# Two-layer graph network on one core: the sums of source and target rows formed by an accumulating gather, and five smaller edits

## The chip, the cores and the metric

The kernel runs on one NeuronCore of a Trainium2 chip. The metric is the time of one execution on the device, in microseconds (us). A core has several engines that run their own instruction lists in order: TensorE (PE in the profile) multiplies matrices into accumulators in PSUM, VectorE (DVE) and ScalarE (ACT) work on rows, GpSimd (POOL) here mostly issues transfers whose addresses come from a list of indices, and SyncE (SP) issues the large loads of weights. They wait for each other by semaphores.

## The reference

There are 625 nodes with 1024 features and 10000 edges from src to dst, sorted by dst. Two layers follow each other, and each has a graph part, a linear attention, and a feed-forward part. Cut to what matters here:

```
xn = layernorm(x)
# layer 0, graph attention: 4 heads of 64, with a self loop for every node
h = rmsnorm(xn) @ W_down
xl, xr = h @ Wl, h @ Wr
msg = xl[src] + xr[dst]
e = einsum('ehd,hd->eh', where(msg > 0, msg, 0.2 * msg), att)
alpha = softmax of e over the edges that have the same dst
g = segment_sum(alpha * xl[src], dst) @ W_up
# linear attention: 16 heads, phi = elu + 1
k, v, q = phi(xn @ Wk), xn @ Wv, phi(xn @ Wq)
m = (q @ (k^T v)) / (q @ sum(k)) @ Wo
x = x + g + m
x = x + ternary_ffn(layernorm(x))
# layer 1
xn = layernorm(x)
x = x + sage(sage(xn)) + linear_attention(xn)   # sage: mean over edges, two products
x = x + attention_and_moe(layernorm(x))         # 8 experts, 2 of them per token
```

## The kernel before, in words

The nodes are 5 tiles of 125. The order of instructions on every engine is written out by hand: a stream object takes for each piece of work its TensorE part and the work that follows it on the other engines, and puts that follow-up one or two steps later. A whole attempt is run once with a plain softmax (the exponentials are not shifted by a maximum); tests collected in `inside` decide at the end whether a second, shifted attempt has to run. With the given data it doesn't.

Layer 0's first stage does the following together.

TensorE computes the keys, values, queries and answers of the linear attention (class `LinearAttention`, L240 to L335). In between, `count` (L418 to L464) multiplies one-hot rows of the edges (bf16, made by VectorE) for 79 blocks of 128 edges into accumulators `pct`, so that a matrix CT of edge counts per pair of nodes results. Two node halves are packed in one number as low + 4096 high. The 79 blocks go in three pieces (up to 27, 53 and 79); after each piece VectorE decodes the accumulators (L448 to L460).

The edge scores are computed in groups of G = 2 columns of 128 edges; 39 groups are full, and the 40th is one column of 16 edges. For a group g POOL fetches rows of xl by src into `ga` and rows of xr by dst into `gb` with indirect transfers (`gather`, L573 to L580). VectorE adds both (L586), applies the leaky relu (L557), multiplies by `att` (L558), reduces per head (L559) and limits the result (L561). ScalarE takes the exponential (L565). POOL scatters it into a table in DRAM at place (src, dst) (`scatter`, L589 to L595). The self loops (`self_loops`, L601 to L608) do the same with rows that are on chip, one node tile at a time, and store the results on the table's diagonal; they also copy xl into `xl1`, which has a 65th column of ones per head.

The pace of the edge work is a plan. `work(us)` is called after every piece of TensorE work with its planned time, and for every 7.6 us it issues one beat g: the self loops of tile g-1 (beats 1 to 5), the exponential of group g-4, the scoring of group g-3, and then column by column on POOL the two gathers of group g and the scatter of group g-5.

When the attention is done, the product px with the output weights follows (L668); VectorE sums the ternary weights (`weight_sums`, L707), POOL loads the table back by target tile (`load_table`, tb), `weigh` multiplies it by the counts (L743), and TensorE forms pg, the weighted sums of the xl1 rows, of which the 65th column is the softmax denominator. Then come seven rounds p = 0 to 6 (`for p in range(NT + 2)`), in which the graph sums of tile p and the feed-forward part of tile p-1 alternate with a `spacer`: two pieces of px in the early rounds, and keys and values of layer 1's attention (`lin1`) from p = 3 on. A key piece writes pk into a small accumulator (`ps1`, of which there are two), adds the bias on VectorE (kb, L247), and takes exp and relu on ScalarE (ke, L249).

After this, layer 1's query loop runs over 8 blocks m; TensorE computes pq, pd and po, and beside them VectorE and ScalarE make the normalized rows of layer 1 and split them into a high and a low part, half a tile at a time (`rows_of`, ten calls, L1072 and L1045 to L1047); at one m VectorE also forms the inverses of the degrees (`inverses`, L1037 to L1041). The rest of the program, from about 850 us on, is the SAGE layers, attention and experts.

Of the kernel before, what the change touches and what calls it, by code (L numbers as in the profile page):

```python
# [33 lines left out]
NB_MIN = 10  # L34
FAR = -1.0e30
LIMIT = 60.0
LEAST, MOST = 1.0e-22, 1.0e25
MAGIC = 12582912.0
BIG = 1.5 * 2.0**35

# [12 lines left out]
def attempt(ctx: ExitStack, tc: tile.TileContext, w: dict, out: bass.AP, shifted: bool):  # L53
# [26 lines left out]
    nc.vector.memset(blockmask[0:64, 0:64], 1.0)  # L80
    nc.vector.memset(blockmask[64:128, 64:128], 1.0)

    inside = const.tile([128, 3], FP, name="inside")
    nc.vector.memset(inside, 1.0)

    def test(col, src, n, pool):
# [128 lines left out]
    class LinearAttention:  # L215


        def __init__(self, xnT, names, bq, work, rows_on):
            self.xnT, self.names, self.work, self.rows_on = xnT, names, work, rows_on
            self.bq = mix.tile([128, KC], FP, tag="bq", name="bq", bufs=2)  # L220
            rows_on.dma_start(out=self.bq, in_=bq)
            self.kv = []
# [15 lines left out]
        def key(self, t):  # L238
            kf, bk, wk = self.kf, self.bk, self.wk

            def pe():
                hold["pk", t] = ps1("pk")
                group(hold["pk", t][:P], [(self.xnT[:, k, nodes(t)], wk(k)) for k in range(KC)])

            def after():
                kb = mix.tile([P, 512], FP, tag="kb", name="kb", bufs=1)
                nc.vector.tensor_tensor(kb, hold.pop(("pk", t))[:P], bk[:P], op=ALU.add)  # L247
                ke = mix.tile([P, 512], FP, tag="ke", name="ke", bufs=1)
                nc.scalar.activation(ke, kb, AF.Exp)  # L249
                nc.scalar.activation(kb, kb, AF.Relu)  # L250
                hold["k", t] = ke, kb

            def after2():
                ke, kb = hold.pop(("k", t))
                nc.vector.scalar_tensor_tensor(kf[:, t, :], ke, 1.0, kb, op0=ALU.min, op1=ALU.add)

            do(None, pe, after, after2)
            self.work(6.9)

        def value(self, t):  # L260
            v, bv, wv = self.v, self.bv, self.wv

            def pe():
                hold["pv", t] = ps1("pv")
                group(hold["pv", t][:P], [(self.xnT[:, k, nodes(t)], wv(k)) for k in range(KC)])

            def after():
                nc.vector.tensor_tensor(v[:, t, :, 0:128],  # L268
                                        hold.pop(("pv", t))[:P].rearrange("p (a b) -> p a b", a=4),
                                        bv[:P].rearrange("p (a b) -> p a b", a=4), op=ALU.add)  # L270

            do(None, pe, after)
            self.work(6.9)
# [64 lines left out]
    with ExitStack() as st0:  # L338
# [8 lines left out]
        with ExitStack() as edges:  # L347
# [51 lines left out]

            pad(xnT)  # L400
            nc.vector.memset(xl1[:, :, :, 64:65], 1.0)

            counting = [(lo, hi, t) for lo, hi in ((0, 27), (27, 53), (53, EN)) for t in range(lo, hi)]
            part = dict(done=0, held=0)
            made_ahead = []

# [10 lines left out]
            def count():  # L419
# [20 lines left out]
                def decode():  # L440
                    for j in range(0, NT, 2):
                        js = slice(j, min(j + 2, NT))
                        n = js.stop - j
                        low, high, v = CT[:, js, 0:HN], CT[:, js, HN:NP], part["pc"][:P, js, :HN]
                        low_r, high_r = CTr[:, js, 0:HN], CTr[:, js, HN:NP]
                        u = pool.tile([P, 2, HN], FP, tag="u", name="u", bufs=1)[:, 0:n, :]

                        nc.vector.tensor_scalar(u, v, 1728.0, BIG, op0=ALU.subtract, op1=ALU.add)  # L448
                        nc.vector.tensor_scalar(u, u, BIG, None, op0=ALU.subtract)
                        if lo == 0:  # L450
                            nc.vector.tensor_tensor(low_r, v, u, op=ALU.subtract)
                            nc.vector.tensor_scalar(high_r, u, 1.0 / 4096, None, op0=ALU.mult)
                        else:
                            nc.vector.scalar_tensor_tensor(high_r, u, 1.0 / 4096, high, op0=ALU.mult, op1=ALU.add)
                            nc.vector.tensor_tensor(u, v, u, op=ALU.subtract)
                            nc.vector.tensor_tensor(low_r, low, u, op=ALU.add)
                    if hi == EN:

                        for s in range(NT):
                            nc.vector.tensor_tensor(CTr[:, s, nodes(s)], CT[:, s, nodes(s)], ident[:P, :P],  # L460
                                                    op=ALU.add)
# [90 lines left out]

            def score(dst, m, n, p):

                nc.vector.scalar_tensor_tensor(m, m, 0.2, m, op0=ALU.mult, op1=ALU.max)  # L557
                nc.vector.tensor_tensor(m, m, att[0:p].unsqueeze(1).to_broadcast([p, n, 256]), op=ALU.mult)  # L558
                nc.vector.tensor_reduce(dst, m.rearrange("p t (h e) -> p t h e", h=4), AX.X, ALU.add)  # L559
                if not shifted:  # L560
                    nc.vector.tensor_scalar(dst, dst, LIMIT, None, op0=ALU.min)  # L561
# [10 lines left out]
            def gather(g, j):  # L572
                lo, n, p = groups[g]  # L573
                if j == 0:
                    ab[g] = [pool.tile([128, G, 256], FP, tag=k, name=k, bufs=4) for k in ("ga", "gb")]
                if j < n:
                    for dst, src, ix in ((ab[g][0], xl_d, si), (ab[g][1], xr_d, di)):
                        nc.gpsimd.indirect_dma_start(  # L578
                            out=dst[0:p, j, :], out_offset=None, in_=src[:, :],
                            in_offset=bass.IndirectOffsetOnAxis(ap=ix[0:p, lo + j:lo + j + 1], axis=0))  # L580

            def score_group(g):
                lo, n, p = groups[g]
                a, b = ab.pop(g)
                m = a[0:p, 0:n, :]
                nc.vector.tensor_tensor(m, m, b[0:p, 0:n, :], op=ALU.add)  # L586
                score(es[0:p, lo:lo + n, :], m, n, p)

            def scatter(g, j):  # L589
                lo, n, p = groups[g]  # L590
# [4 lines left out]
                        in_=es[0:p, lo + j, :], in_offset=None)  # L595

            own = pool.tile([P, NT, 4], FP, name="own")

            diagonal = table[0:N * (N + 1), :].rearrange("(s d) h -> s d h", d=N + 1)[:, 0, :]

            def self_loops(t):  # L601

                m = pool.tile([P, 1, 256], FP, tag="xd", name="gs", bufs=1)
                nc.vector.tensor_tensor(m[:, 0, :], xlr[:, t, 0:256], xlr[:, t, 256:512], op=ALU.add)
                score(own[:, t:t + 1, :], m, 1, P)
                exp(own[:, t:t + 1, :])
                nc.vector.tensor_copy(xl1[:, t, :, 0:64], xlr[:, t, 0:256].rearrange("p (h e) -> p h e", h=4))
                rows_dma(nc.scalar, diagonal[nodes(t), :], own[:, t, :])  # L608


# [1 line left out]

            def work(us):
                beat["us"] += us
                while beat["us"] >= 7.6 * beat["g"] and beat["g"] < len(groups) + 5:
                    g = beat["g"]
                    beat["g"] += 1
                    if 1 <= g <= NT:
# [6 lines left out]
                    for j in range(G):  # L625
                        if g < len(groups):
                            gather(g, j)
                        if g >= 5:
                            scatter(g - 5, j)

            work(0.0)
            states = []
# [55 lines left out]
            nc.sync.dma_start(out=wu, in_=w["W_up"].rearrange("(k p) n -> p k n", p=128))  # L688
            bo = [lin.bias(w["L0_bo"], c, tag) for c, tag in enumerate(("bk_t", "bv_t"))]
            do.flush()  # L690
            while beat["g"] < len(groups) + 5:
                work(8.0)

        xpool = ctx.enter_context(tc.tile_pool(name="xpool", bufs=1, side="right", reuse_waits="tile"))
        x = xpool.tile([P, NT, D], FP, name="x")
# [265 lines left out]
        for p in range(NT + 2):  # L961
# [11 lines left out]
            if p == 0:  # L973
                xnT1 = bigT("xnT1")
                nc.gpsimd.memset(xnT1[:, :, N:NP], 0.0)
                lin1 = LinearAttention(xnT1, ("L1_Wq", "L1_Wk", "L1_bk", "L1_Wv", "L1_bv"), w["L1_bq"],
                                       lambda us: None, nc.gpsimd)
            if p < NT:
                sums(p)
            if 1 <= p <= NT:  # L980
# [37 lines left out]
    def degrees():  # L1018
# [8 lines left out]
        def after():  # L1027
            nc.vector.tensor_scalar(halves(dinv), hold["pdeg"][:, :, :HN], 1.0, None, op0=ALU.max)
            if not shifted:
                most = sage.tile([128, 1], FP, name="most")  # L1030
                nc.vector.tensor_reduce(most, dinv, AX.X, ALU.max)
                nc.vector.tensor_scalar(inside[:, 1:2], most, 4095.0, None, op0=ALU.is_le)

        do(None, pe, after)

# [40 lines left out]
    for m in range(KC - 1):  # L1076
        lin1.query(m + 1)
        lin1.answer(m, oT)
        for _ in range(2 if m < 4 else 1):
            if rows_left:  # L1080
                rows_of(*rows_left.pop(0))
        if m == 5:
            inverses()
    assert not rows_left
    for name in ("b1", "L1_bo"):
# [513 lines left out]
    def ranks():  # L1599
        hold["prt"] = ps1("prt")  # L1600
        group(hold["prt"][:P, 0:NT * NE], [(before, flat)])
        group(hold["prt"][:P, NT * NE:2 * NT * NE], [(ones[:P, :P], flat)])
        group(hold["prt"][:P, 2 * NT * NE:2 * NT * NE + 3], [(ones[:, :P], inside)])

    do(None, ranks)
    ptot = hold["prt"][:, NT * NE:2 * NT * NE]
# [48 lines left out]
    nc.vector.tensor_reduce(exp_f, blk, AX.X, ALU.add)  # L1655
    meta = pool.tile([P, NB + 2], I32, name="meta")
    within = pool.tile([P, 1], FP, name="within")
    nc.vector.tensor_reduce(within, hold["prt"][:P, 2 * NT * NE:2 * NT * NE + 3], AX.X, ALU.add)
    nc.vector.tensor_scalar(meta[:, NB + 1:NB + 2], within, -1.0, 384.0, op0=ALU.mult, op1=ALU.add)
    nc.vector.tensor_scalar(meta[:, 0:NB], exp_f, float(NE - 1), None, op0=ALU.min)  # L1660
    nc.vector.tensor_copy(meta[:, NB:NB + 1], ends[3][:, NE - 1:NE])
    hidden(3)
# [71 lines left out]
    rest(NB_MIN)  # L1734
    again = None
    if not shifted:
        again = nc.values_load(meta[0:1, NB + 1:NB + 2], min_val=0, max_val=384,
                               skip_runtime_bounds_check_because="384 less three sums of up to 128 ones and zeros")


    with tc.manual_schedule(engines={mybir.EngineType.PE, mybir.EngineType.DVE, mybir.EngineType.Pool}):
# [121 lines left out]
```

## Time and profile before

| what | value |
|---|---|
| median of 3 runs | 2243.34 us (2241.93 to 2249.37) |
| the profiled execution's own time | 2241.98 us |
| its span in the profile | 2240.2 us |
| mean granted TensorE clock | 0.977 |
| TensorE busy | 2124.3 us, 95% |
| VectorE busy | 754.2 us, 34% |
| ScalarE busy | 193.5 us, 9% |
| POOL busy | 346.7 us, 15% |

The span is what the profile covers; 1.8 us of the execution lie outside of it. Times of instructions are in us from the span's start. In the profile a line of a timeline gives the start, the duration, the engine, the line of the kernel, the operation, what it writes and reads, and in brackets how long the engine stood idle before it and what ended that. A line of a group of instructions gives the number of instructions, their busy time in us and the mean in ns, and the idle time before them. In the slices of the span each digit is the busy share in tenths of one fortieth, 56 us. The TensorE clock may be granted in part only, which lengthens its products.

### The profile page before, as it was taken

What the parts mean: (1) busy time and instruction counts of PE and PEld (TensorE: products, weight loads), DVE (VectorE), ACT (ScalarE), POOL (GpSimd) and SP (SyncE); (2) the same over time, 40 slices, a digit from 0 to 9 for tenths busy, and PEclk for the clock granted to TensorE, in tenths of its full rate; (3) what the DMA queues carried; (4) which work ended last, traced back from release to release, by engine and by line L of the source; (5) the groups of instructions that cost most, each with busy time, mean ns of one, the idle gap of its engine ahead of it and who ended that gap; (6) DMA issues with size and microseconds to landing.
All of it is one profiled execution on the core that took longest, in us unless ns stands there. A gap on an engine that the chain in (4) does not pass through costs nothing. (4 is left out here: it accounts for less than half of the span.)

```text
span 2240.2 us, 17398 instructions
## 1 busy us (share of the span) xinstructions
PE 2124.3 (95%) x6934; PEld 1214.5 (54%) x6934; DVE 754.2 (34%) x1265; ACT 193.5 (9%) x349; POOL 346.7 (15%) x351
## 2 busy tenths in 40 slices
PE   7997889798899989999999999999999999999998
PEld 5564455354554657764445767556754444444443
DVE  4878668666421580000113124322111111111112
ACT  2000011011110210000000111110000000000000
POOL 1667767400000040010000000110000000000010
PEclk9998999898899999999999999999999999999999
DMA  9452252431122110231212111030198997998742
GB/s 282 126 179 64 65 187 86 111 89 43 38 85 75 47 48 1 75 141 38 75 38 103 38 38 38 19 103 33 62 337 320 333 331 278 326 332 294 268 147 93
DMA packets 145849, 301.63 MB, mean 135 GB/s; under 512 B 12370, under 2 KB 22436, under 8 KB 145754
## 3 DMA queue, kind: packets, MB, share of 16 engines
q1 hardware_dynamic: 123412, 243.18, 30.4%
q0 software_dynamic: 17664, 47.47, 7.1%
q10 hardware_dynamic: 4678, 9.72, 1.4%
q8 instruction: 58, 0.95, 0.2%
q14 instruction: 37, 0.30, 0.0%
HBM read 277.49 MB, written 22.84 MB: 134 GB/s over the span
## 5 line engine op out<-in xcount | busy, mean ns | idle before, releaser
L129 PE MATMUL pu<-w,xgT 128*128 128x512 f32 x768 | 333.9, 593 | 1.9 <-DVE xgT L1157 1.9
L129 PEld LDWEIGHTS pu<-w,xgT 128*128 128x128 f32 x768 | 144.0, 190 | 174.8 <-issue 172.0
L129 PE MATMUL pyb<-w,hb 128*128 128x512 f32 x384 | 174.3, 598 | 2.5 <-ACT yb L104 2.1
L129 PE MATMUL pq<-xnT,w 128*128 128x313 f32 x512 | 143.2, 440 | 11.0 <-DVE v L268 9.7
L129 PE MATMUL pk<-w,xnT 128*125 128x512 f32 x320 | 141.0, 593 | 4.7 <-DVE x L909 4.7
L129 PE MATMUL pv<-w,xnT 128*125 128x512 f32 x320 | 140.7, 592 | 1.2 <-ACT xnT L925 1.2
L129 PE MATMUL p<-tT,w 128*128 128x313 f32 x512 | 136.3, 428 | 0.4 <-DVE tT L1157 0.4
L129 PEld LDWEIGHTS pq<-xnT,w 128*128 128x128 f32 x512 | 99.8, 196 | 54.1 <-DVE v L268 10.5
L1697 DVE TENSOR_TENSOR su<-pu,su 128x512 f32<-128x512 f32 x24 | 16.6, 691 | 314.6 <-ACT su L1696 314.6
L129 PEld LDWEIGHTS pyb<-w,hb 128*128 128x128 f32 x384 | 69.8, 189 | 90.9 <-issue 74.8
L129 PEld LDWEIGHTS p<-tT,w 128*128 128x128 f32 x512 | 96.8, 190 | 37.9 <-issue 1.2
L129 PEld LDWEIGHTS pk<-w,xnT 128*125 128x125 f32 x320 | 59.3, 187 | 78.7 <-issue 72.0
L129 PEld LDWEIGHTS pv<-w,xnT 128*125 128x125 f32 x320 | 59.4, 188 | 72.4 <-issue 70.5
L592 POOL DMA_INDIRECT table<-es,at x79 | 88.3, 1118 | 63.7 <-DMA table<-es,at 32.6
L1680 POOL DMA_INDIRECT xg<-rows_d,slots x12 | 11.4, 947 | 524.7 <-PE pxg L1687 449.0
L578 POOL DMA_INDIRECT gb<-xr_d,di x79 | 81.7, 1034 | 24.1 <-issue 24.1
L578 POOL DMA_INDIRECT ga<-xl_d,si x79 | 80.1, 1014 | 30.9 <-issue 20.1
L668 PE MATMUL px<-w,oT 128*125 128x512 f32 x160 | 75.6, 629 | 8.1 <-DVE oT L333 6.5
L1047 DVE TENSOR_TENSOR z<-pz,z 125x512 fp32r<-125x512 f32 x10 | 6.9, 692 | 196.8 <-ACT z L1045 196.8
L129 PE MATMUL px<-w,hT 128*125 128x512 f32 x160 | 70.3, 592 | 0.0
L129 PE MATMUL px<-w,oT 128*125 128x512 f32 x160 | 70.3, 592 | 0.0
L129 PE MATMUL ph<-meanT,w 128*128 128x313 f32 x256 | 70.1, 426 | 0.0
(359 smaller groups left out, 2572.0 us busy)
## 6 DMA issues: line engine op xcount, KB each, us to landing
w<-in_eW_dram SPq DMA_DIRECT2D x144, 1024.0 KB
w<-in_L_Wk_dram SPq DMA_DIRECT2D x8, 1024.0 KB
w<-in_L_Wv_dram SPq DMA_DIRECT2D x8, 1024.0 KB
w<-in_L_Wq_dram SPq DMA_DIRECT2D x8, 1024.0 KB
w<-in_L_Wo_dram SPq DMA_DIRECT2D x8, 1024.0 KB
w<-in_W_self_dram SPq DMA_DIRECT2D x8, 1024.0 KB
w<-in_W_neigh_dram SPq DMA_DIRECT2D x8, 1024.0 KB
w<-in_sW_dram SPq DMA_DIRECT2D x8, 1024.0 KB
```

What stands on the lines that cost most here:

```text
L129: nc.tensor.matmul(dst, lhsT=lhsT, rhs=rhs, start=(i == 0), stop=(i == len(pairs) - 1))
L578: nc.gpsimd.indirect_dma_start(out=dst[0:p, j, :], out_offset=None, in_=src[:, :], in_offset=bass.IndirectOffsetOnAxis(ap=ix[0:p, lo + j:l ...
L592: nc.gpsimd.indirect_dma_start(out=table[:, :], out_offset=bass.IndirectOffsetOnAxis(ap=at[0:p, lo + j:lo + j + 1], axis=0), in_=es[0:p, l ...
L668: nc.tensor.matmul(hold["px", t][:P, c, :], lhsT=oT[:, k, nodes(t)], rhs=wo[c](k), start=(k == 0), stop=False)
L1047: nc.vector.tensor_tensor(low, src, high.bitcast(FP), op=ALU.subtract)
L1680: nc.gpsimd.indirect_dma_start(out=xg, out_offset=None, in_=rows_d[:, :], in_offset=bass.IndirectOffsetOnAxis(ap=slots[:, b:b + 1], axis=0))
L1697: nc.vector.tensor_tensor(su, pu[:, 0, :], su, op=ALU.mult)
```

## The change

It has six parts. (1) `gb` goes; the rows of xr are added by a transfer with an add of its own, `add_targets`, into `ga`, which has 6 buffers instead of 4. It is issued one beat after the plain gather of the same group. (2) The leaky relu of m is written as 0.2 m + 0.8 max(m, 0). Per edge only the second part is left: one operation, max with zero and multiply by att (scaled by 0.8 beforehand). Of the first part, what belongs to the target cancels in the softmax; what belongs to the source becomes a weight exp(0.2 att . xl) on the source's row in `xl1`, computed in `self_loops`. A test on this weight is added. (3) The counts of all 79 blocks stay in the accumulators and are decoded once; the test of it is extended. (4) The keys and values of `lin1` use the larger accumulators (`ps2`, three of them). (5) The scatter comes 4 instead of 5 beats after the gather. (6) The query loop of layer 1 takes three `rows_of` per step while there are any (3, 3, 3, 1) instead of two and then one (2, 2, 2, 2, 1, 1), and the inverses come at m = 4 instead of 5.

The diff, cut to its core:

```diff
-LEAST, MOST = 1.0e-22, 1.0e25
+LINEAR = 20.0
+LEAST, MOST = 1.0e-22, 1.0e16
...
-    inside = const.tile([128, 3], FP, name="inside")
+    inside = const.tile([128, 4], FP, name="inside")
...
-                hold["pk", t] = ps1("pk")
+                hold["pk", t] = ps2("pk")[:, 0, :] if self.large else ps1("pk")
...
-                hold["pv", t] = ps1("pv")
+                hold["pv", t] = ps2("pv")[:, 0, :] if self.large else ps1("pv")
...
+            if not shifted:
+                nc.vector.tensor_scalar(att, att, 0.8, None, op0=ALU.mult)
-            counting = [(lo, hi, t) for lo, hi in ((0, 27), (27, 53), (53, EN)) for t in range(lo, hi)]
+            counting = [(lo, hi, t) for lo, hi in (((0, 27), (27, 53), (53, EN)) if shifted else ((0, EN),))
+                        for t in range(lo, hi)]
...
-                nc.vector.scalar_tensor_tensor(m, m, 0.2, m, op0=ALU.mult, op1=ALU.max)
-                nc.vector.tensor_tensor(m, m, att[0:p].unsqueeze(1).to_broadcast([p, n, 256]), op=ALU.mult)
+                by_att = att[0:p].unsqueeze(1).to_broadcast([p, n, 256])
+                if shifted:
+                    ...
+                else:
+                    nc.vector.scalar_tensor_tensor(m, m, 0.0, by_att, op0=ALU.max, op1=ALU.mult)
...
-                    ab[g] = [pool.tile([128, G, 256], FP, tag=k, name=k, bufs=4) for k in ("ga", "gb")]
+                    ab[g] = pool.tile([128, G, 256], FP, tag="ga", name="ga", bufs=6)
                 if j < n:
-                    for dst, src, ix in ((ab[g][0], xl_d, si), (ab[g][1], xr_d, di)):
-                        nc.gpsimd.indirect_dma_start(
-                            out=dst[0:p, j, :], out_offset=None, in_=src[:, :],
-                            in_offset=bass.IndirectOffsetOnAxis(ap=ix[0:p, lo + j:lo + j + 1], axis=0))
+                    nc.gpsimd.indirect_dma_start(
+                        out=ab[g][0:p, j, :], out_offset=None, in_=xl_d[:, :],
+                        in_offset=bass.IndirectOffsetOnAxis(ap=si[0:p, lo + j:lo + j + 1], axis=0))
+            def add_targets(g, j):
+                lo, n, p = groups[g]
+                if j < n:
+                    nc.gpsimd.indirect_dma_start(
+                        out=ab[g][0:p, j, :], out_offset=None, in_=xr_d[:, :],
+                        in_offset=bass.IndirectOffsetOnAxis(ap=di[0:p, lo + j:lo + j + 1], axis=0),
+                        compute_op=ALU.add)
 
             def score_group(g):
                 lo, n, p = groups[g]
-                a, b = ab.pop(g)
-                m = a[0:p, 0:n, :]
-                nc.vector.tensor_tensor(m, m, b[0:p, 0:n, :], op=ALU.add)
-                score(es[0:p, lo:lo + n, :], m, n, p)
+                score(es[0:p, lo:lo + n, :], ab.pop(g)[0:p, 0:n, :], n, p)
...
+            def test_linear():
+                c = pool.tile([P, NT, 4], FP, name="clipped")
+                nc.vector.tensor_scalar(c, linear, -4.0 * LINEAR, 4.0 * LINEAR, op0=ALU.max, op1=ALU.min)
+                nc.vector.tensor_tensor(c, c, linear, op=ALU.is_equal)
+                nc.vector.tensor_reduce(inside[:P, 3:4], c, AX.XY, ALU.min)
...
-                nc.vector.tensor_copy(xl1[:, t, :, 0:64], xlr[:, t, 0:256].rearrange("p (h e) -> p h e", h=4))
+                rows = xlr[:, t, 0:256].rearrange("p (h e) -> p h e", h=4)
+                if shifted:
+                    nc.vector.tensor_copy(xl1[:, t, :, 0:64], rows)
+                else:
+                    nc.vector.tensor_tensor(m[:, 0, :], xlr[:, t, 0:256], att[:P], op=ALU.mult)
+                    nc.vector.tensor_reduce(linear[:, t, :], m.rearrange("p t (h e) -> p (t h) e", h=4), AX.X, ALU.add)
+                    part4 = pool.tile([P, 4, 1], FP, tag="part4", name="part4", bufs=2)
+                    nc.vector.tensor_scalar(part4[:, :, 0], linear[:, t, :], -4.0 * LINEAR, 4.0 * LINEAR,
+                                            op0=ALU.max, op1=ALU.min)
+                    nc.scalar.activation(xl1[:, t, :, 64:65], part4, AF.Exp, scale=0.25)
+                    nc.vector.tensor_tensor(xl1[:, t, :, 0:64], rows,
+                                            xl1[:, t, :, 64:65].to_broadcast([P, 4, 64]), op=ALU.mult)
...
-                while beat["us"] >= 7.6 * beat["g"] and beat["g"] < len(groups) + 5:
+                while beat["us"] >= 7.6 * beat["g"] and beat["g"] < len(groups) + 4:
...
-                        if g >= 5:
-                            scatter(g - 5, j)
+                        if 1 <= g < len(groups) + 1:
+                            add_targets(g - 1, j)
+                        if g >= 4:
+                            scatter(g - 4, j)
...
+                lin1.large = True
...
+                nc.vector.tensor_reduce(most, hold["pdeg"][:, :, :HN], AX.XY, ALU.add)
+                nc.vector.tensor_scalar(most, most, float(E), None, op0=ALU.is_equal)
+                nc.vector.tensor_tensor(inside[:, 1:2], inside[:, 1:2], most, op=ALU.mult)
...
-        for _ in range(2 if m < 4 else 1):
+        for _ in range(3):
             if rows_left:
                 rows_of(*rows_left.pop(0))
-        if m == 5:
+        if m == 4:
             inverses()
```

What is left out turns `inside`'s three sums into four where they are read, and the constant of the decoding from 1728 to 2047.

## The prediction

> **What bounds the kernel now.** I read the page from the slices down.
>
> ```profile
> PE   7997889798899989999999999999999999999998
> DVE  4878668666421580000113124322111111111112
> POOL 1667767400000040010000000110000000000010
> PEclk9998999898899999999999999999999999999999
> ```
>
> A slice is 56 us. TensorE is busy everywhere; what it lacks is mostly in the first eight slices (to 448 us), the only place where VectorE and POOL are busy too. So I ask what ends that stage. Of the costliest groups, POOL's three indirect transfers per column of edges:
>
> ```profile
> L592 POOL DMA_INDIRECT table<-es,at x79 | 88.3, 1118 | 63.7 <-DMA table<-es,at 32.6
> L578 POOL DMA_INDIRECT gb<-xr_d,di x79 | 81.7, 1034 | 24.1 <-issue 24.1
> L578 POOL DMA_INDIRECT ga<-xl_d,si x79 | 80.1, 1014 | 30.9 <-issue 20.1
> ```
>
> These are 237 instructions, 250 us busy. POOL's timeline from 92.45 us (first scatter) to 387.89 has 204 of them without a pause but 0.30 us between two and about 24 us in which a scatter waits for the one before it: (296.3 - 24)/204 = 1.33 us each. VectorE waits for them (its waits, 60 to 450 us):
>
> ```profile
> DVE ga L586 <- DMA gb<-xr_d,di: 54.1, 13, 10.9
> ```
>
> At the end the two timelines, POOL and then VectorE, show the chain (start, duration; the wait in brackets):
>
> ```profile
> 373.82 0.94 POOL L578 DMA_INDIRECT gb<-xr_d,di  x1 [0.30 <-issue]
> ...
> 384.17 0.95 POOL L578 DMA_INDIRECT gb<-xr_d,di  x1 [0.30 <-issue]
> ...
> 417.91 1.78 POOL L592 DMA_INDIRECT table<-es,at  x1 [1.91 <-DMA table<-es,at]
> 421.40 0.89 POOL L163 DMA_DIRECT2D tb<-table  x1 [1.70 <-DMA table<-es,at]
> ```
>
> ```profile
> 380.31 0.69 DVE L586 TENSOR_TENSOR ga<-ga,gb 128x512 f32<-128x512 f32 x1 [4.14 <-DMA gb<-xr_d,di]
> ...
> 397.92 0.81 DVE L333 TENSOR_TENSOR oT<-po,z 128x626 f32<-128x626 f32 x1
> ```
>
> Rows gathered at 373.82 let group 37 be scored at 380.31; behind that VectorE makes the last attention output oT(7), for which TensorE waits before px. So POOL's pace sets the stage's end, through VectorE's order. Later TensorE is 95% busy and waits only at small places; I return to the rounds of the FFN.
>
> **What the Trainium skill says.** "DMA: Bandwidth & Descriptors", SWDGE vs HWDGE vs iDMA: only GpSimd's transfers can accumulate; no price is given. "GPSIMD Engine Reference", When to use GPSIMD: one core of a pair emits the read descriptors, the other the write ones; an accumulating row has its destination to read as well. No run so far shows one. "SBUF — State Buffer", SBUF: two separate sides: VectorE and GpSimd share a port under an exclusive lock; the trace agrees in kind: a gather takes 0.95 us alone and up to 1.3 to 1.45 beside scoring. "TensorE: Matmul & The Clock Gate", Part 1: an idle window of some 3.4 us halves the clock; the trace agrees: in the FFN rounds, behind such waits, the 40 products of pg take 7.31 us where without them they take 4.48.
>
> **The change, part by part.**
>
> *Targets added by the gather.* Out goes the add at L586, 39 x 0.68 + 0.40 = 27 us of VectorE. POOL's count stays 237: 79 plain gathers, 79 accumulating ones, 79 scatters. But the second gather of a group moves one beat back, six POOL instructions or 8 us, as it must wait for the first to land (2.8 us in the median, so POOL, with all later gathers and scatters behind, should not stand there). Group 37's rows, complete after the instruction at 373.82, are then complete after the slot at 384.17: 384.17 + 0.95 + 3.4 of landing = 388.5 instead of 380.3. From there to the end of oT(7) were 18.4 us (380.31 to 398.7); two groups' scoring there gets shorter by two of its operations each (next part), 2 x 1.4, leaving 15.6: 404.1, so +5.5.
>
> Let d be what an accumulating transfer takes POOL more than a plain one. Trace: nothing. Below: 0, since a negative one has no reason (the same rows, one read more). Above: a 16-row gather takes 0.86, a 128-row one 0.95, so rows cost little beyond a fixed part; doubling the row part (0.1 on 112 rows) gives 0.1; doubling half the instruction 0.5. I take 0.15. Some 75 of them lie in front of the slot: 75 x 0.15 = +11.
>
> *Split leaky relu.* Scoring drops one pass (L557 and L558 become one), 40 x 0.69 = 27 us of VectorE. Each of the 5 self loops gains about 1.3 us (two passes of 0.42, small ones, a multiply of 0.42 for a copy of 0.29, less one pass), 6.5 us, plus 0.5 for the test: VectorE, early in the stage, ahead of POOL's first scatters, which wait for the self loops' stores (84.5 and 92 us): start 0 to +1.5, taken +1. The scaling of att at the head of VectorE's list waits for its load, 0 to +1, hidden by TensorE's later wait for wd (15.96). With two of three two-input passes gone, POOL is disturbed less: its 226 instructions stand 18 us over their floors (0.95 and 1.00), and the three passes make up about 11 of it; half, -5. From 0 to -11.
>
> *One decoding.* Two of three decodings go: 7.1 + 9.9 = 17 us of VectorE, and TensorE's waits for them (12.6 us at L455). In the stage's middle; the end hangs on POOL, so TensorE arrives earlier at its waits for oT. At nothing; without the cover, -12. The test of the sum (about 1 us) falls where VectorE is idle.
>
> *Scatter lag 4.* The scatters stay as many; 7 instead of 11 are left at the end, each 2.9 us: the table's load would go from 421.4 to 421.4 - 4 x 2.9 + 5 + 11 d/0.15, about 415 to 425. In the kernel before, TensorE reached the table's use right at its landing (px ends 430.7, pg starts 430.68). With px 2 to 13 later this is not late. A scatter now follows its exp within a beat; where VectorE runs behind, in the first 150 us, POOL would wait: within the start's 0 to 1.5.
>
> Stage: +5.5 + 1 - 5 = +1.5, plus 75 d.
>
> *Keys in large accumulators.* In rounds 3 to 5, of which this is one, in TensorE's timeline and ScalarE's:
>
> ```profile
> 511.82 7.13 PE L129 MATMUL pk<-w,xnT 128*125 128x512 f32 x16 [1.43 <-DVE x L909]
> ...
> 521.32 0.65 PE L924 MATMUL ptr<-ident,xn 125*128 125x125 f32 x4 [1.93 <-DVE kb L247]
> 523.12 7.31 PE L129 MATMUL pg<-xl,pT 125*125 125x65 f32 x40 [1.16 <-ACT xnT L925]
> ```
>
> ```profile
> 521.30 0.63 ACT L249 ACTIVATE ke<-kb 125x512 f32<-125x512 f32 x1 [2.80 <-DVE kb L247]
> 522.50 1.05 ACT L925 ACTIVATE xnT<-ptr 128x500 f32<-128x500 f32 x2
> ```
>
> pk no longer waits for a buffer (1.43), but pg waits for ScalarE's copy, which stands behind ke, that behind kb on VectorE (520.58), and this behind the row work that begins when the last product ends at 510.4. This chain does not move: TensorE stands once for about 4.5 us instead of three times. Nothing there. In round 6, with no pg behind, its waits of 1.16 and about 1 before pv go: -2.2, against +0.4 for what comes behind it, taken -2.
>
> *Three rows per query step, inverses earlier.* The loop of layer 1's queries runs at VectorE's pace: from one qf to the next 11.84 us (757.06, 768.90), of which two rows take 1.85 each; TensorE's own work is 10.55. From 745.11 to 823.62 six steps take 78.5. After: three steps of three rows, 11.84 + 1.85 = 13.7 each; a step of one row and one of none at TensorE's 10.55; the step with the inverses (808.52 to 816.1, 7.6 us, in place of the rows) 11.84 - 3.7 + 7.6 = 15.7: 77.9, so -0.6. Two rows at 794.73 and 806.32 took 1.6 more each, beside additions on POOL; rows done sooner may escape that: -0.5 to -3, taken -1.5.
>
> Sum: +1.5 - 2 - 1.5 + 11 = +9. The profiled execution took 1.8 us more than its span: 2241.98; so 2251. The median of the runs shown, 2243.34, is 1.4 above it: 2252. From no change a measurement of this kernel can tell about 0.3%, 6.7 us.
>
> **The rivals.** *Accumulating costs POOL nothing* (d = 0). For it: the row part is small beside the fixed one. Then 2242 - 2 = 2240, no change. Against: the second read has to be described by someone. Chance 0.27. *Faster: TensorE in the FFN rounds stops waiting and keeps its clock.* Place: the three rounds from 511, 549 and 587 us; if the row work came early enough, each would lose its 4.5 us of waits, and pg would take 4.48 (its time at full clock) instead of 7.31: 3 x (4.5 + 2.8) = 22 us, 2252 - 22 = 2230. For it: pk and kb do come earlier. Against: the queue through ke. It decides from 16 of the 22 us. Chance 0.18, with d = 0 and POOL's relief at its full 11 instead of 5 (2234) counted in. *Accumulating is dear*, d = 0.5: 75 x 0.35 more, +26: 2278; the same if landing takes longer than the 8 us that the beat gives, since then POOL stands in front of its own gathers. Chance 0.15. *The tests fail*, and the second attempt runs: time about doubles. The tests are wider than the usual data; 0.01.
>
> **How the numbers follow.** My forecast, d about 0.1 to 0.25, has 0.39 and gives 2247 to 2260; its likeliest is 2252. Slower: 0.39 with the dear case 0.15 and 0.01, 0.55. Same 0.27, faster 0.18. For 8 in 10 the range goes from 2233, which leaves out some two thirds of the faster case (0.12), to 2282, just over the dear one, beyond which I leave 0.06.
>
> **What the profile after would show.** The accumulating gather's row gives d directly: 1.03 us in the mean is d = 0, 1.5 is the dear case. The L586 add gone and scoring waiting for the accumulating transfer instead, oT(7) ending near 404 + 75 d - 4. Seven scatters in the tail. pg still at about 7.3 us in the three rounds, behind one longer wait. If POOL's pace falls under 1.25 us, or TensorE shows no wait for oT, POOL was not the bound and I am wrong.

## The result

The changed kernel takes 2273.19 us (median of 4 runs, 2271.77 to 2273.74), the kernel before 2245.93 (4 runs, 2241.93 to 2249.37): a ratio of 1.0132, 95% interval 1.0116 to 1.0149. That is slower by 27 us, inside the range, 21 us above the likeliest value. The profiled execution has a span of 2271.3 us against 2240.2, so +31.1. A second pair of measurements, told with the experiments, turned the sign round: what the kernel before takes depends on where or when it runs.

The slices of the span after, one digit for 57 us:

```profile
PE   7977867798889989999999999999999999999998
DVE  5744335756532383000012133332011111011112
POOL 1777877620000040001000000020000000000010
```

VectorE is less busy in the first eight slices, and POOL more, and for longer. POOL's three transfers per column, as groups (busy us, mean ns, then the idle time before them):

```profile
L596 POOL DMA_INDIRECT ga<-xr_d,di x79 | 127.9, 1619 | 27.1 <-issue 25.0
L608 POOL DMA_INDIRECT table<-es,at x79 | 81.8, 1035 | 49.1 <-DMA table<-es,at 28.7
L588 POOL DMA_INDIRECT ga<-xl_d,si x79 | 79.2, 1003 | 31.3 <-issue 22.4
```

The accumulating gather takes 1.62 us of POOL, where the plain one of the same rows took 1.03: d is 0.585, and 79 x 0.585 = 46.2 us. The scatters got 6.5 us shorter in all and the other gathers 0.9, so POOL's work is 38.8 us longer. VectorE's waits show who sets the pace (total, times, longest, 60 to 450 us); before it was 54.1 us in 13 waits:

```profile
DVE ga L569 <- DMA ga<-xr_d,di: 166.1, 35, 10.4
```

TensorE's timeline after, at the places where the prediction's steps stand: px behind the last answer, pg at the start of the rounds, and the first round with a key piece.

```profile
439.03 4.33 PE L705 MATMUL px<-w,oT 128*125 128x512 f32 x6 [4.01 <-DVE oT L335]
...
469.68 4.48 PE L130 MATMUL pg<-xl,pT 125*125 125x65 f32 x40
...
543.53 7.13 PE L130 MATMUL pk<-w,xnT 128*125 128x512 f32 x16 [0.46 <-DVE x L848]
550.50 1.02 PE L963 MATMUL ptr<-ident,xn 125*128 125x125 f32 x8
555.81 8.24 PE L130 MATMUL pg<-xl,pT 125*125 125x65 f32 x40 [4.29 <-ACT xnT L964]
```

Against the kernel before, px stands 40.3 us later (398.78), pg 39.0 (430.68), the first pk 31.7 (511.82). From there to the degree counts (pdeg, 661.89 and 693.78) nothing more moves (+31.9), the query loop gives 0.8, and the rest of the program takes the same. So all of the loss is made before 439 us, and 7.3 us of it come back between pg and pk: pg runs through in 4.48 us without waiting, where before it had four waits of 0.5 for pT and the px behind it took 8.44 instead of 7.08.

### The profile page after: what moved, and what is told of

Its sections match the earlier page's. It is cut to its first block, busy times and chain, and to the rows that moved or that the text cites. A ratio compares the mean times of both kernels' runs of the same rounds, so it can differ in the third digit from the quotient of the medians.

```text
span 2271.3 us, 17245 instructions
## 1 busy us (share of the span) xinstructions
PE 2131.5 (94%) x6934; PEld 1220.2 (54%) x6934; DVE 685.4 (30%) x1172; ACT 194.5 (9%) x354; POOL 391.2 (17%) x351
## 5 line engine op out<-in xcount | busy, mean ns | idle before, releaser
L130 PE MATMUL pq<-xnT,w 128*128 128x313 f32 x512 | 144.9, 443 | 21.0 <-DVE v L270 20.3
L596 POOL DMA_INDIRECT ga<-xr_d,di x79 | 127.9, 1619 | 27.1 <-issue 25.0
L608 POOL DMA_INDIRECT table<-es,at x79 | 81.8, 1035 | 49.1 <-DMA table<-es,at 28.7
L705 PE MATMUL px<-w,oT 128*125 128x512 f32 x160 | 75.2, 626 | 5.6 <-DVE oT L335 4.0
L569 DVE SCALAR_TENSOR_TENSOR ga<-ga,att 128x512 f32<-128x512 f32 (+1 forms) x40 | 27.4, 684 | 166.1 <-DMA ga<-xr_d,di 166.1
L442 PE MATMUL pct<-ring 128*125 128x313 bf16 x395 | 59.9, 309 | 12.4 <-DVE ring L421 12.4
```

The source lines that it names most:

```text
L130: nc.tensor.matmul(dst, lhsT=lhsT, rhs=rhs, start=(i == 0), stop=(i == len(pairs) - 1))
L442: nc.tensor.matmul(part["pc"][:P, j, :HN], lhsT=os[:, nodes(j)], rhs=od[:, :HN], start=(t == lo), stop=(t == hi - 1))
L569: nc.vector.scalar_tensor_tensor(m, m, 0.0, by_att, op0=ALU.max, op1=ALU.mult)
L596: nc.gpsimd.indirect_dma_start(out=ab[g][0:p, j, :], out_offset=None, in_=xr_d[:, :], in_offset=bass.IndirectOffsetOnAxis(ap=di[0:p, lo + ...
L608: nc.gpsimd.indirect_dma_start(out=table[:, :], out_offset=bass.IndirectOffsetOnAxis(ap=at[0:p, lo + j:lo + j + 1], axis=0), in_=es[0:p, l ...
L705: nc.tensor.matmul(hold["px", t][:P, c, :], lhsT=oT[:, k, nodes(t)], rhs=wo[c](k), start=(k == 0), stop=False)
```

## The experiments

Five theories were put on record. A: only POOL's longer instruction costs time. B: the later place and landing of the added rows cost it. C: one of the other parts does. D and E came up after the first runs, about stretches in which TensorE stands without a wait that the profile explains. D: POOL's plain transfers at their full rate bring them on. E: they belong to the chip, or to something else in the kernel before. The kernels ran in three groups; those of a group share a chip and the runs of the kernel before. In the first two groups the kernel before took 2287.17 and 2285.60 us, in the third 2243.45, as where the prediction was made. I call the former place Q and the latter P. The chip of the first group has the number 0, that of the second and of the third the number 1. So Q is not one chip, and whether Q and P differ by the chip or by the time isn't known.

**First group, at Q: the accumulation taken out, undone, and alone.**

e1_plain_second, an edit to the changed kernel. The source rows are missing in the scores.

```diff
-                        in_offset=bass.IndirectOffsetOnAxis(ap=di[0:p, lo + j:lo + j + 1], axis=0),
-                        compute_op=ALU.add)
+                        in_offset=bass.IndirectOffsetOnAxis(ap=di[0:p, lo + j:lo + j + 1], axis=0))
```

> The changed kernel, but the second transfer of a column overwrites ga instead of accumulating into it; order, lags, buffers and waits stay. It leaves the source rows out of the scores. Theory A (POOL's own time for an accumulating transfer, 1.62 us against 1.03, sets the stage): the group of the second transfer falls to 1.00 to 1.06 us, POOL's chain gets 79 x 0.58 = 46 us shorter, some 6 of which the scatters take back, and the time is 2227 to 2237. Theory B (the second transfer's place one beat behind the first, and the data's later landing, make VectorE wait): 2260 or more, with VectorE still waiting some 150 us for ga. Theory C (the smaller lag of the scatters, or one of the other parts, costs the time): 2260 or more, too.

Measured: 2278.78 us, 0.9942 of the kernel before (0.9919 to 0.9965). The second transfer fell to 0.97 us and VectorE's waits for ga to 38.9, as A says of POOL, but the time didn't follow. TensorE stood 42 us for nothing that the profile shows. The profile calls such a wait "issue".

e2_two_gathers, the changed kernel with its first part undone:

```diff
-    ab[g] = pool.tile([128, G, 256], FP, tag="ga", name="ga", bufs=6)
+    ab[g] = [pool.tile([128, G, 256], FP, tag=k, name=k, bufs=4) for k in ("ga", "gb")]
...
+    nc.vector.tensor_tensor(m, m, b[0:p, 0:n, :], op=ALU.add)
...
-    if 1 <= g < len(groups) + 1:
-        add_targets(g - 1, j)
```

> The changed kernel with the first part undone: both gathers in one beat into ga and gb, the add on VectorE; the other five parts stay. Theory A: POOL's pace is that of the kernel before or a little better, as one pass of the scoring is gone; 2228 to 2236, and it beats the kernel before by 8 to 15 us, since the tail of scatters is also four shorter. Theory B: the same or a few us less than e1_plain_second's time, and clearly below it (5 us or more) if the landing matters at all. Theory C: 2260 or more.

Measured: 2278.74 us, 0.9966 (0.9945 to 0.9987), with 47 us of unexplained standing.

e3_add_alone, the kernel before with this part alone (gather, add_targets, six buffers; the lag of the scatters stays 5):

```diff
...
-    nc.vector.tensor_tensor(m, m, b[0:p, 0:n, :], op=ALU.add)
...
+    if 1 <= g < len(groups) + 1:
+        add_targets(g - 1, j)
     if g >= 5:
         scatter(g - 5, j)
```

> The kernel before with the first part alone (accumulating gather one beat later, six buffers, no add on VectorE); leaky relu, decodings and lag 5 as before. Theory A: 79 x 0.58 = 46 us on POOL's chain, and the table's tail of 11 scatters still behind it: 2278 to 2292, so slower than all six parts together (2273). Theory C: the other parts carry the loss, so this one is at 2245 to 2262.

Measured: 2274.35 us, 0.9932 (0.9903 to 0.9961), and no unexplained standing at all. Its accumulating gather takes 1.63 us, its px starts and its rounds run as in the changed kernel within 2 us (first pk 545.48). Its span, 2272.6, stands 1.3 above that of the changed kernel and 32 above that of the kernel before at P: one part alone carries nearly all of it, though the numbers come from two places.

e4_relu_alone, the kernel before with the split leaky relu and its test alone (of the edit, the scoring):

```diff
-    nc.vector.scalar_tensor_tensor(m, m, 0.2, m, op0=ALU.mult, op1=ALU.max)
-    nc.vector.tensor_tensor(m, m, att[0:p].unsqueeze(1).to_broadcast([p, n, 256]), op=ALU.mult)
...
+    nc.vector.scalar_tensor_tensor(m, m, 0.0, by_att, op0=ALU.max, op1=ALU.mult)
```

> The kernel before with the split leaky relu alone (and its test). Theory A with POOL disturbed by VectorE's passes over two inputs: POOL's 237 transfers get 3 to 8 us shorter in all and the time is 2236 to 2241. If VectorE's passes don't disturb POOL: 2242 to 2246, as VectorE waits for POOL at the end anyway. If the self loops' longer work delays POOL's first scatters: up to 2248.

Measured: 2288.26 us, 1.0000 (0.9980 to 1.0021), 57 us of standing. POOL's three groups of transfers take 242.1 us busy, where the kernel before takes 244.9 at Q (b1, below): the relief is 3 us between these two profiles, and it bought nothing there.

The ranges of this group were laid for a kernel before at 2243. At Q e1, e2 and e4 miss theirs, and e3 ends 4 us under that of A. So the times of this group can't choose between A, B and C.

**Second group, at Q again: what the standing is.** The kernels before and after unchanged, and e1 and e2 once more.

> The kernel before, unchanged, to have its profile beside the experiments. In the first experiments it took 2287 us on their chip, against 2243 where the prediction was made, and the profiles of the kernels with plain gathers showed TensorE standing for 20 to 50 us between single products with nothing that it waited for ('issue'). If that is a matter of the chip: 2243 to 2246 here with no such standing, or about 2287 with 20 to 50 us of it between 60 and 450 us.

> The changed kernel, unchanged. Theory A (POOL's instruction time alone): 2271 to 2275 on either kind of chip, as its POOL is slower and TensorE isn't disturbed; so slower than before by 27 to 30 us where the kernel before takes 2244, and faster by some 13 us where that takes 2287. If the chip slows everything: 2310 or more where the kernel before takes 2287.

> As e1_plain_second: the changed kernel with a second transfer that overwrites instead of accumulating, so that the source rows are missing in the scores. Where TensorE shows no unexplained standing: theory A 2227 to 2237, theories B and C 2260 or more. Where it does: 2274 to 2283, as in the first run.

> As e2_two_gathers: the changed kernel with the first part undone. Where TensorE shows no unexplained standing: theory A 2228 to 2236, faster than the kernel before by 8 to 15 us; theory C 2260 or more. Where it does: 2271 to 2289, as in the first run.

Measured: the kernel before 2283.07 us, 0.9991 (0.9970 to 1.0011); the changed kernel 2271.28, 0.9949 (0.9929 to 0.9969); e1b 2279.27, 0.9958 (0.9941 to 0.9975); e2b 2278.56, 0.9969 (0.9950 to 0.9989). The changed kernel takes at Q what it takes at P. The kernel before takes 40 us more there, and that is where the sign comes from. In its profile at Q, TensorE's waits (60 to 450 us) and a piece of its timeline:

```profile
PE pct L437 <- issue: 39.3, 41, 2.4
```

```profile
256.31 0.42 PE L437 MATMUL pct<-ring 128*125 128x313 bf16 x1 [1.68 <-issue]
258.44 0.42 PE L437 MATMUL pct<-ring 128*125 128x313 bf16 x1 [1.70 <-issue]
261.24 0.42 PE L437 MATMUL pct<-ring 128*125 128x313 bf16 x1 [2.38 <-issue]
```

The same products at P, in the kernel before:

```profile
146.22 4.16 PE L437 MATMUL pct<-ring 128*125 128x313 bf16 x30
```

There, 30 products take 4.16 us; at Q one comes every 1.4 to 2.8 us, in stretches of up to 32 us, while the profile names nothing that TensorE waits for. In all, 48.0 us of such waits (b1), 41.3 (e1b), 39.5 (e2b), 42.3, 47.1 and 56.7 (e1, e2, e4), and none in the two kernels with accumulating gathers (a1, e3), nor in any profile taken at P.

TensorE isn't alone in this. VectorE stands as well, for semaphores whose release the profile puts down to no instruction ("remote"): 66.1 us in b1 and 40 to 94 in the other five (60 to 450 us), none in a1 and e3 nor at P. The longest, of 29.5 us, lies in the stretch shown above and ends at 266.15:

```profile
DVE kb L247 <- remote: 40.3, 2, 29.5
```

POOL meanwhile goes on issuing without a pause until 262.0, when it has to wait 12.2 us for VectorE's scoring. TensorE's last wait of that stretch ends at 264.7. The six profiles have twelve stretches of ten or more such waits of TensorE, less than 6 us apart. All twelve end some 1 to 4 us after POOL begins a pause of more than 1 us; in eleven it is POOL's first such pause since the stretch began. This speaks for D. But it is an order in time and no test, and POOL's issuing alone is not enough: at P, in the kernel before, POOL issues from 166.6 to 288.3 us without such a pause, and nothing stands.

**Third group, at P: POOL slowed by hand.** Its main ranges were laid for Q. A memset on POOL behind the two transfers of a column lengthens its column and changes nothing that is computed.

```diff
+            idle = pool.tile([128, 780], FP, name="idle")
...
+                    nc.gpsimd.memset(idle, 0.0)
```

p1_before_slow has 780 elements on the kernel before, p4_before_half 430, p3_plain_slow 780 on e1 (source rows missing in the scores), p2_two_slow 430 on e2.

> The kernel before with a memset of 780 elements on POOL behind each pair of gathers, which should lengthen POOL's column by some 0.55 us, about what an accumulating transfer costs more. Theory D (TensorE's unexplained standing is brought on by POOL's plain transfers following each other at their full rate): the standing between 60 and 450 us falls from some 45 us to under 10, and the kernel gets faster by what it does more, 2268 to 2278 where the kernel before takes 2285. Theory E (the standing belongs to the chip, or to something else in the kernel before): the standing stays and POOL's 43 us come on top or hide behind it: 2285 to 2330. On a chip where the kernel before doesn't stand (2243): 2278 to 2288.

> The kernel before with a memset of 430 elements at the same place, about 0.27 us per column. Theory D: if the rate alone decides, the standing is gone or halved, 2255 to 2275 where the kernel before takes 2285. Theory E: 2283 to 2305. On a chip without standing: 2258 to 2266.

> The changed kernel with a second transfer that overwrites instead of accumulating (so the source rows are missing in the scores), and a memset of 780 elements on POOL behind it, so that POOL's column takes about as long as with the accumulation. Theory A (of the accumulation only POOL's time counts): 2268 to 2278, the changed kernel's own time, with TensorE's standing gone and VectorE waiting some 150 us for ga again. If the accumulation costs by its landing too: 5 us or more below the changed kernel. If TensorE still stands (theory E): 2285 or more.

> The changed kernel with two plain gathers and the add on VectorE (first part undone), and a memset of 430 elements on POOL per column. Theory D: standing gone or halved, 2245 to 2266, faster than both kernels on a chip where they take 2285 and 2271. Theory E: 2278 to 2300. On a chip without standing: 2245 to 2258.

| kernel | memset, us | median, us | ratio (95%) | px | pg | first pk | span |
|---|---|---|---|---|---|---|---|
| before | none | 2243.45 | | 398.78 | 430.68 | 511.82 | 2240.2 |
| p4, before | 0.495 | 2265.48 | 1.0094 (1.0077 to 1.0111) | 412.01 | 446.67 | 529.39 | 2257.7 |
| p1, before | 0.766 | 2282.44 | 1.0165 (1.0148 to 1.0182) | 434.25 | 470.64 | 553.93 | 2282.7 |
| p2, changed, two gathers | 0.485 | 2253.30 | 1.0040 (1.0031 to 1.0050) | 416.71 | 449.24 | 523.66 | 2250.6 |
| p3, changed, plain second | 0.766 | 2274.35 | 1.0132 (1.0115 to 1.0149) | 439.12 | 471.08 | 545.01 | 2272.3 |
| after | none | 2273.19 | 1.0132 (1.0116 to 1.0149) | 439.03 | 469.68 | 543.53 | 2271.3 |

(px is the start behind the last answer; the places of the rows without memset come from their profiles at the prediction.)

All four fall in the ranges laid for a place without standing. p3 tells the accumulation from POOL's time. A plain transfer and an idle POOL give the changed kernel's time to 1.2 us, with px, pg and pk within 1.5 us and a wait of VectorE of nearly the same size. POOL's groups, one column of its timeline, and that wait:

```profile
L598 POOL DMA_INDIRECT ga<-xr_d,di x79 | 77.9, 987 | 26.6 <-issue 26.6
L601 POOL MEMSET idle<- 128x780 f32 x79 | 60.5, 766 | 0.0
```

```profile
91.65 0.95 POOL L598 DMA_INDIRECT ga<-xr_d,di  x1 [0.30 <-issue]
92.60 0.76 POOL L601 MEMSET idle<- 128x780 f32 x1
93.53 1.01 POOL L610 DMA_INDIRECT table<-es,at  x1 [0.17 <-issue]
```

```profile
DVE ga L569 <- DMA ga<-xr_d,di: 153.9, 31, 10.6
```

The scatter starts 0.17 us behind the memset, where it starts 0.30 behind a transfer, so the memset of 0.766 lengthens the column by about 0.64, close to the 0.585 that the accumulation adds. The accumulating transfer lands 3.9 us after its start in the median, a plain one 2.8. So this later landing costs nothing that can be measured beside POOL's time. The place one beat behind is another matter, for p3 keeps it. In p1, which has both gathers in one beat and the same memset, px stands 4.9 us earlier than in p3; but p2 has the placing of p4, and its px stands 4.7 us later than that of p4. So whether the place or another part costs these 5 us isn't shown. Of the 40 us by which px moved, 35 are in p1, which has neither the accumulation nor any other part. And the kernel before pays for POOL's time with and without accumulation: two doses gave +22 and +39 us. Theory C, that another part carries the loss, falls too. At equal idle time the changed kernels are faster than the kernel before, by 12.2 us (p2 against p4, 7.1 in the spans) and 8.1 us (p3 against p1, 10.4 in the spans): the other five parts gain. Beside the accumulating gather itself they gain less: the span of e3 is 1.3 us above that of the changed kernel at P and 3.7 above that at Q (a1, 2268.9). The timelines say where they gain: between pg and pk p1 takes 83.3 us and p3 73.9. In p1, as in the kernel before and p4, VectorE's wait for the table's load makes TensorE stand in front of pg:

```profile
DVE pT L746 <- DMA tb<-table: 14.5, 1, 14.5
```

The changed kernel has no such wait, and p2, whose gathers are placed as in p4 and whose tail is four scatters shorter, has one of 8.0 us that ends as px does (pg to pk 74.4 us, against 82.7 in p4). So the smaller lag seems to gain there, though no run has it alone. It isn't all of it: e3, with the long tail, also takes 75.2, as its px is itself a beat later.

D was not tried where it matters, as none of these kernels met a place with standing. That plain gathers bring the standing on is what six profiles with it and two without agree on at Q; whether it is POOL's rate, and what differs between P and Q, stays open. Nor was the changed kernel with two gathers and no memset run at P. From p2 and p4 it should take 7 to 12 us less than the kernel before there; that is an estimate. Of the kernels here none was measured to beat both at both places.

## Why the prediction was right, and where not

**The bound.** Right. POOL's pace sets the stage's end, through the rows that VectorE waits for; p1, p4 and p3 show it without any accumulation.

**The price of an accumulating gather.** This is the term that failed. "I take 0.15", with 0.5 as the upper bound: it measured 0.585, above both. I had priced a second read of the rows as a doubled row part (0.1 us for 112 rows). POOL's timeline after has both sizes, 128 rows and 16, of the plain and of the accumulating gather:

```profile
414.84 0.97 POOL L588 DMA_INDIRECT ga<-xl_d,si  x1 [0.30 <-issue]
416.12 1.58 POOL L596 DMA_INDIRECT ga<-xr_d,di  x1 [0.31 <-issue]
...
421.25 0.87 POOL L588 DMA_INDIRECT ga<-xl_d,si  x1 [0.30 <-DVE ga L569]
...
429.17 1.36 POOL L596 DMA_INDIRECT ga<-xr_d,di  x1 [0.30 <-issue]
```

The row part did double, from 0.10 to 0.22. What I had no row for is a fixed part of 1.36 - 0.87 = 0.49 us. With 0.585 the prediction's sum is +1.5 - 2 - 1.5 + 75 x 0.585 = +42, and the span grew by 31. Put on the median of 2243, +42 would be 2285, outside the range. So that the measured time lies inside is in part luck: gains that the sum didn't have hid a part of the error.

**The stage.** With the measured d it gives +1.5 + 44 = 45; px moved by 40.3. POOL's relief was taken as 5; the scatters and plain gathers got 7.4 shorter. What became of the +5.5 for the place isn't separated, as said above.

**The tail of scatters.** "With px 2 to 13 later this is not late" was right for the kernel after and priced at nothing, which was wrong for the kernel before: there the table was the later of the two. VectorE's wait of 10 us for tb stood in its profile, and I took the meeting of px's end and pg's start as balance. With the seven scatters, as forecast, and the later px 7.3 us came back behind pg. Of the error in d, 75 x 0.435 = 33 us, 11 were hidden: some 5 in the stage, 2.4 of them the larger relief, and the rest here.

**One decoding.** At nothing, and nothing speaks against it, but no run has this part alone. TensorE's 12.6 us of waits for the decoding went, and its waits for v grew, whose additions stand behind the scoring on VectorE: that of pq from 9.7 to 20.3, that of pkv from none to 12.1. p1, with three decodings and POOL slowed, has 18.7 for the decoding and 21.9 of pq, so waits of this size go with POOL's longer stage.

**Large accumulators.** The merged wait of "about 4.5 us instead of three times" measured 4.29, 5.01 and 5.01. The three rounds were taken at nothing; from the first pk to the pk of round 6 they took 103.4 us instead of 101.1. The waits of pk and of what stands behind it come to 14.8 us instead of 13.2, and pg behind them takes 8.24 and 8.66 instead of 7.31 and 8.66, at a granted clock of 0.50 to 0.54 between 556 and 564 us. Round 6 gave 2.1, as forecast: +0.2 together, where -2 was taken.

**Query loop.** Taken -1.5, measured -0.8; the three steps of 13.7 to 13.9 are there (qf at 777.00, 790.80, 804.67, 818.37).

**The rivals.** Of these the dear one came true, d = 0.5 with 2278, given 0.15. That it costs POOL nothing is refuted. TensorE in the FFN rounds didn't stop waiting; the 22 us put on that counted pg in three rounds, and the third (from 587 us) has none. Right in range and sign, the forecast gave most weight to a d that was too small by a factor of four. And it didn't foresee that the sign holds only at P.

## What to carry to other kernels

Where one engine's issue of transfers sets the pace, moving arithmetic into its transfers can make the bound dearer. Here 27 us of additions left VectorE, which waited anyway, and 46 us came to POOL. An idle instruction of known length on the suspected engine measures what its time is worth, and put in place of a suspected cost it shows whether anything else counts. Where two things meet, such as the end of px and the table's landing, look at both engines' waits before calling it a balance.

## What was not expected of the hardware

The accumulating gather moves rows one by one. The packet counts and the queue of POOL's transfers, before and then after:

```profile
DMA packets 145849, 301.63 MB, mean 135 GB/s; under 512 B 12370, under 2 KB 22436, under 8 KB 145754
...
q0 software_dynamic: 17664, 47.47, 7.1%
```

```profile
DMA packets 153335, 301.61 MB, mean 133 GB/s; under 512 B 12370, under 2 KB 32420, under 8 KB 153242
...
q0 software_dynamic: 25152, 47.47, 8.8%
```

For the same bytes there are 9984 = 78 x 128 more packets under 2 KB, and 7488 = 78 x 96 more on POOL's queue: 128 packets of one row (1 KB) where a full column's plain gather had 32 of four rows. This doesn't seem to be what costs POOL its half microsecond: the 78 full columns make up the whole difference, so the transfer of 16 rows has no packet more than before, and it has the fixed part of 0.49 us as well.

The other surprise is the standing of TensorE at Q: single products at intervals of 1.4 to 2.8 us, with no wait recorded, while VectorE stands too and POOL issues plain indirect transfers without a pause. The kernel before takes 40 us more there.
